# The residual of a convolution-attention layer: from TensorE transposes to a second load that VectorE turns over, with the input normalised two strips at a time

## The chip, the cores and the metric

The kernel runs on one core of one Trainium2 chip. The metric is the device time of one execution in microseconds; the times compared are medians of several executions.

## The reference, cut to what matters

The input `x` has 256 channels on a 64 x 64 image, 4096 tokens, in float32. Three stages follow one another, and each adds to a residual stream.

```python
# layer 0: group normalisation, box-window linear attention, projection
x = x + _L0_conv_ref(_gn(x), Wq, Wk, Wv, Wout, bout)
#   k, q = sigmoid(W x);  v = W x, normalised per head;  windows of 64, 32 and 16
#   out  = einsum(q, box(k v)) / (einsum(q, box(k)) + 1e-6);  Wout out + bout
# layer 1: attention and a mixture of 8 experts on tokens
t = _to_tokens(x)                      # [4096 tokens, 256 channels]
t = t + _L1_attn_ref(_ln_t(t), ...)
t = t + _L1_ffn_ref(_ln_t(t), ...)
```

What concerns this change is `x + ... + bout`: the residual, in float32, is the plain input with the output bias of the first layer added, and later stages want it with tokens on the partitions, while `x` arrives with channels on the partitions.

## The kernel before, in words

One function computes all three stages in order, and tiles of SBUF and PSUM come from pools. A scheduler decides the order of the instructions on each engine from the order in which they are written and from its own estimate of when they become ready. Each engine then works through its own queue strictly in that order and waits on semaphores. When a tile reuses the buffer of an older one (the same `tag` in a pool), its first writer waits for the older tile's last reader.

**Layout.** The image is cut into 8 strips of 8 columns (`NCH`, `SW`) and 4 blocks of 16 rows (`NB`, `BH`). A strip in a block has 128 pixels, one tile of tokens; tile `4 * strip + block` of `t` (128 tokens by 256 channels and 8 more columns) holds the residual. `act` holds the normalised input, channels on partitions, strip after strip.

**The start (L232 to L294).** `x` is loaded in eight pieces of 512 KB over two DMA queues (L237). The residual is built at once (L243 to L266): GpSimd gathers a block's pixels strip by strip into `block` (L248), TensorE transposes 128 x 128 squares into PSUM against the identity (L256), and the result goes to `t` with the bias row `bout` added: for the first two blocks by VectorE (L263), for the other two by a ScalarE copy (L265) and a GpSimd addition (L266). Beside this, VectorE takes the statistics of each channel (`bn_stats`, L273; `bn_aggr`, L274), TensorE averages them over groups of 8 channels (L276, L284), and VectorE normalises `x` into `act` with one instruction for each half of the channels (L287), all strips in one.

**prepare(g)**, called for the two groups of four heads. L309 to L332: for four tiles at a time, which is one strip, eight products of `act` with the weights of k and v (L314) fill a pair of PSUM banks; ScalarE's sigmoid takes k (L322), VectorE copies v (L323), GpSimd squares it (L324), VectorE sums the squares (L325). Every 16 tiles a square root (L328), a reciprocal (L330) and a multiplication (L332) normalise v. Three such pairs of banks (`two_banks`, L300) are used in turn, here and in all that follows in `prepare`.

Then, strip by strip (L418 to L442), products with constant matrices give running sums of k over an area of the image (L422, L426), which VectorE adds to what came before (L430, L433, L435). After the first strip TensorE also sums k times v over each cell of 64 pixels, in 512 small products (`sum_cells`, L360); ScalarE copies these to `st` (L369), and VectorE works on them between the area blocks (L378 to L398, the generator `near`). L341 then projects q and k by channel, with ScalarE's sigmoid behind (L348), into `qk`. That tile has the tag of `x`, so it takes the buffer that `x` had. ScalarE and VectorE form differences of the areas (`tall`, L464 to L469), VectorE multiplies them by q (L488), and L491 sums these products into the denominators.

**After that**, `attend` computes the window attention and adds each result to `t` (L714); attention on tokens follows, and then the experts and the output.

Of the kernel before, what the change touches and what calls it, by code (L numbers as in the profile page):

```python
# [10 lines left out]

# [1 line left out]

# [1 line left out]

# [5 lines left out]
F32 = mybir.dt.float32  # L23
BF16 = mybir.dt.bfloat16
I32 = mybir.dt.int32
AF = mybir.ActivationFunctionType
ALU = mybir.AluOpType
# [3 lines left out]
P = 128  # L31
C = 256
KC = C // P
N = 4096
NT = N // P
CH = 512
NCH = N // CH
IMG = 64
SW = 8
BH = 16  # L40
NB = IMG // BH
CELL = SW * SW
D = 32
# [68 lines left out]
def tile_conv_attn_hybrid(ctx: ExitStack, tc: tile.TileContext, a: dict, out: bass.AP):  # L112
    nc = tc.nc
# [32 lines left out]
    def row_on_all(name, n, pool):  # L146
        got = pool.tile([P, n], F32, name=f"{name}_all")
        nc.scalar.dma_start(got, a[name].partition_broadcast(P))
        return got
# [36 lines left out]
    with ExitStack() as phase:  # L186
# [23 lines left out]
        with (  # L210
            tc.tile_pool(name="c_x", bufs=1) as small,
            psum("c_ps0", 2) as ps,
        ):
            bank, _ = banks(ps)
            cst.update(constants_of("c", small))
            group = cst["group"]

            def masks(to, ys, n, kind):
                xm = cst["xmask"][:, SW * kind : SW * (kind + 1)]
                nc.gpsimd.tensor_mul(  # L220
                    to.rearrange("p n (y c) -> p (n y) c", c=SW),
                    ys.unsqueeze(2).to_broadcast([P, SW * n, SW]),
                    xm.unsqueeze(1).to_broadcast([P, SW * n, SW]),
                )

            for kind in range(2):
                masks(mask[:, kind], cst["ymask"], ncell, kind + 1)
            masks(mask0, cst["ymask"][:, SW * _MCELL0[-1] :], _MCELLS[-1], 0)
            masks(ycut, cst["ycut"], 2, 0)


            x = big.tile([P, KC, N], F32, tag="qk", name="x")  # L232
            xr = a["x"].rearrange("(k p) n -> p k n", p=P)
            for i in range(4):
                for k in range(KC):
                    at = slice(i * N // 4, (i + 1) * N // 4)
                    (nc.sync if k else nc.scalar).dma_start(x[:, k, at], xr[:, k, at])  # L237
            bout = row_on_all("L0_conv_bout", C, wts)
            first = weights(0)
            ck = constants_of("k", wts)  # L240


            ximg = x.rearrange("p k (y x) -> p k y x", x=IMG)  # L243
            tb = t.rearrange("p (i b) c -> p b i c", b=NB)
            for b in range(NB):
                block = small.tile([P, KC, NCH, P], F32, name="block", bufs=2)
                for k in range(KC):
                    nc.gpsimd.tensor_copy(  # L248
                        block[:, k].rearrange("p i (y c) -> p y i c", c=SW),
                        ximg[:, k, BH * b : BH * (b + 1), :].rearrange("p y (i c) -> p y i c", c=SW),  # L250
                    )
                for ix in range(0, NCH, 2):
                    tp = bank("tp")
                    for i in range(2):
                        for k in range(KC):
                            nc.tensor.transpose(  # L256
                                tp[:, C * i + P * k : C * i + P * (k + 1)], block[:, k, ix + i, :], ident
                            )

                    to, tp = tb[:, b, ix : ix + 2, :C], tp.rearrange("p (i c) -> p i c", c=C)  # L260
                    by = bout.unsqueeze(1).to_broadcast([P, 2, C])
                    if b < NB // 2:
                        nc.vector.tensor_add(to, tp, by)  # L263
                    else:
                        nc.scalar.copy(to, tp)  # L265
                        nc.gpsimd.tensor_add(to, to, by)  # L266


            stats = small.tile([P, KC, NCH, 6], F32, name="stats")
            mv = small.tile([P, KC, 2], F32, name="mv")  # L270
            for k in range(KC):
                for i in range(NCH):
                    nc.vector.bn_stats(stats[:, k, i, :], x[:, k, chunk(i)])  # L273
                nc.vector.bn_aggr(mv[:, k, :], stats[:, k].rearrange("p i s -> p (i s)"))  # L274
            mean_ps = bank()
            nc.tensor.matmul(mean_ps[:, :KC], group, mv[:, :, 0], start=True, stop=True)  # L276
            mean = small.tile([P, KC], F32, name="mean")
            nc.vector.tensor_copy(mean, mean_ps[:, :KC])
            off = small.tile([P, KC], F32, name="off")
            nc.vector.tensor_sub(off, mv[:, :, 0], mean)  # L280
            nc.vector.tensor_mul(off, off, off)
            nc.vector.tensor_add(off, off, mv[:, :, 1])
            var_ps = bank()
            nc.tensor.matmul(var_ps[:, :KC], group, off, start=True, stop=True)  # L284
            rstd = rstd_of(small, var_ps[:, :KC], KC, 1e-5)
            for k in range(KC):
                nc.vector.tensor_scalar(  # L287
                    act[:, k].rearrange("p (i y c) -> p y i c", y=IMG, c=SW),
                    x[:, k].rearrange("p (y i c) -> p y i c", y=IMG, c=SW),
                    mean[:, k : k + 1],  # L290
                    rstd[:, k : k + 1],
                    op0=ALU.subtract,
                    op1=ALU.mult,
                )  # L294

        def prepare(g, prep, ps):

# [11 lines left out]
            for i4 in range(0, NT, 4):  # L309
                pr = two_banks()  # L310
                kv = pr.rearrange("p j (i n o) -> p (j i) n o", i=2, n=2)
                for i in range(4):
                    for k in range(KC):
                        nc.tensor.matmul(  # L314
                            kv[:, i],
                            act[:, k, tok(i4 + i)],
                            w3[:, k, 1:3, :],
                            start=k == 0,
                            stop=k == KC - 1,
                        )  # L320
                at = slice(i4, i4 + 4)
                nc.scalar.activation(kt[:, at, :], kv[:, :, 0, :], AF.Sigmoid)  # L322
                nc.vector.tensor_copy(v[:, at, :], kv[:, :, 1, :])  # L323
                nc.gpsimd.tensor_mul(sq[:, at, :], v[:, at, :], v[:, at, :])  # L324
                nc.vector.tensor_reduce(ss[:, 4 * i4 : 4 * (i4 + 4)], heads(sq[:, at, :]), AX.X, ALU.add)  # L325
                if i4 % 16 == 12:
                    half = slice(4 * (i4 - 12), 4 * (i4 + 4))
                    nc.scalar.sqrt(ss[:, half], ss[:, half])  # L328
                    nc.vector.tensor_scalar_max(ss[:, half], ss[:, half], 1e-12)
                    nc.vector.reciprocal(ss[:, half], ss[:, half])  # L330
                    to = heads(v[:, i4 - 12 : i4 + 4, :])
                    nc.vector.tensor_mul(to, to, ss[:, half].unsqueeze(2).to_broadcast([P, 2 * NT, D]))  # L332

            qk = big.tile([P, 2, N], F32, tag="qk", name="qk")

            def by_channel(n, i):

# [80 lines left out]
            for ix in range(NCH):  # L418
                pr = two_banks()
                for m in range(NB):  # L420
                    lhsT = kt[:, NB * ix + m, :]
                    nc.tensor.matmul(  # L422
                        pr[:, 0, P * m :], lhsT, ck["before8"][:, : CH - P * m], start=m == 0, stop=m == NB - 1
                    )
                    n = SW + IMG + 1
                    nc.tensor.matmul(  # L426
                        pr[:, 1, :n], lhsT, ck["sides"][:, n * m : n * (m + 1)], start=m == 0, stop=m == NB - 1
                    )
                left = side.unsqueeze(2).to_broadcast([P, IMG + 1, SW])
                nc.vector.tensor_add(  # L430
                    area[:, ix, :IMG, :], pr[:, 0, :].rearrange("p (y c) -> p y c", c=SW), left[:, :IMG]
                )
                nc.vector.tensor_add(area[:, ix, IMG, :], pr[:, 1, :SW], left[:, IMG])  # L433
                upto = new_side()
                nc.vector.tensor_add(upto, pr[:, 1, SW:n], side)  # L435
                side = upto
                if ix == 0:

                    sum_cells()
                for _ in range(3 if ix else 0):  # L440
                    next(steps, None)
            for _ in steps:  # L442
                pass
            for i in range(0, NCH, 2):
                by_channel(0, i)
            later = [lambda i=i: by_channel(1, i) for i in range(0, NCH, 2)]
# [672 lines left out]
    with ExitStack() as phase:  # L1119
# [49 lines left out]
        with ExitStack() as routing:  # L1169
# [7 lines left out]
            at = 0  # L1177
# [303 lines left out]
```

## Time and profile before

The median of three runs is 2946.89 us (2946.64 to 2948.19). The profiled execution spans 2947.3 us.

| Engine | busy, us | share of the span |
|---|---|---|
| TensorE | 2807.9 | 95% |
| VectorE | 2079.4 | 71% |
| ScalarE | 1526.5 | 52% |
| GpSimd | 740.8 | 25% |

A share is an average over stages, so the first 140 us, to which the change belongs, are also read as stretches. Here are the busy microseconds of each engine and the clock granted to TensorE, as a part of full speed.

| stretch, us | TensorE | VectorE | ScalarE | GpSimd | clock |
|---|---|---|---|---|---|
| 20 to 34 | 11.05 | 12.22 | 6.12 | 11.17 | 0.76 |
| 34 to 62 | 28.00 | 12.55 | 8.56 | 13.33 | 1.00 |
| 62 to 78 | 12.80 | 5.65 | 3.79 | 1.04 | 0.79 |
| 78 to 97 | 19.00 | 16.52 | 3.33 | 0.00 | 1.00 |
| 97 to 140 | 37.26 | 29.41 | 13.45 | 0.00 | 0.95 |

The first stretch has the transposes and the normalisation, the second the products for k and v, the third the cell sums, the fourth the areas, and the last the projections and denominators. A row of the timeline shown further on gives the start, the time from the first start to the last end of a merged group, the engine, the line, the operation, the result and its sources with their shapes, and the number of instructions; in brackets stands the idle time before it and what ended it. PEld is TensorE's weight load. A row of the windows gives the stretch and its length, then each engine's busy time with its number of instructions (PE, PEld, VectorE, ScalarE, GpSimd), then the clock, the DMA share and GB/s.

### The profile page before, as it was taken

How to read it: one execution, taken by the hardware profiler on the slowest of the kernel's cores; microseconds unless marked ns; L12 is line 12 of the kernel's file. 1: busy time of each engine (PE TensorE's matmuls, PEld its weight loads, DVE VectorE, ACT ScalarE, POOL GpSimd, SP SyncE). 2: the span in 40 equal slices, each digit the busy share in tenths (PEclk: the TensorE clock that was granted, in tenths of full speed). 3: DMA queues.
4: the chain of work that ended last, by engine and by line, in shares of the span. 5: the costliest groups of instructions: out<-in, count | busy, mean ns of one | idle time of the engine just before them, and what ended most of it. 6: DMA issues, size and time to landing. Idle time of an engine off the chain costs nothing.

```text
span 2947.3 us, 63169 instructions
## 1 busy us (share of the span) xinstructions
PE 2807.9 (95%) x26422; PEld 1359.9 (46%) x26422; DVE 2079.4 (71%) x2975; ACT 1526.5 (52%) x2110; POOL 740.8 (25%) x832
## 2 busy tenths in 40 slices
PE   7899999889999989999999999999999689999996
PEld 5456442645644354222222222222222268888884
DVE  5776777577676886999999999999999821111113
ACT  2242324124232312888888888888888622222222
POOL 4085758108585711000000000000000022222220
PEclk9999999999999999999999999999999879999997
DMA  2000000000000000000000000000000155665665
GB/s 86 6 2 4 3 2 2 7 1 3 3 2 3 1 18 1 1 8 6 5 5 5 5 5 5 5 5 5 5 5 5 41 190 189 197 196 188 190 202 197
DMA packets 92634, 133.29 MB, mean 45 GB/s; under 512 B 16914, under 2 KB 73976, under 8 KB 92340
## 3 DMA queue, kind: packets, MB, share of 16 engines
q1 hardware_dynamic: 78008, 101.12, 10.5%
q0 software_dynamic: 6912, 18.88, 2.3%
q10 hardware_dynamic: 7420, 9.15, 0.9%
q8 instruction: 211, 3.46, 0.5%
q14 instruction: 83, 0.68, 0.1%
HBM read 111.00 MB, written 18.12 MB: 44 GB/s over the span
## 4 chain that ended last, share of the span: by engine, by line
PE 57%; DVE 1%; DMA 1%; ACT 1%; issue 1%; POOL 0%; SPq 0%; POOLq 0%; ACTq 0%; DVEq 0%
PE ps_two L970 20%; PE ps_acc L938 17%; PE ps_hp L1395 9%; PE ps_yp L1402 8%; PE ps_den L919 1%; PE ps_den L938 1%; DMA y<-yrows 1%; PE ps_tp L1370 1%; PE ps_acc L1319 1%; ACT z L1203 1%; DVE t L1439 0%; DVE total L987 0%; DMA yrows<-y,target 0%; DVE rec L1016 0%; DMA xs<-zrows,source 0%
## 5 line engine op out<-in xcount | busy, mean ns | idle before, releaser
L980 ACT ACTIVATE pe<-ps_two 128x1024 f32<-128x1024 f32 x1024 | 993.2, 1022 | 153.9 <-PE ps_two L970 148.7
L987 DVE TENSOR_TENSOR total<-total,pe 128x1024 f32<-128x1024 f32 x928 | 1058.1, 1215 | 3.3 <-ACT pe L980 3.3
L970 PE MATMUL ps_two<-qk 32*128 32x512 f32 x4096 | 631.8, 641 | 3.1 <-POOLq L925 1.9
L938 PE MATMUL ps_acc<-pe,v 128*32 128x512 f32 x4096 | 548.2, 606 | 0.1
L533 ACT COPY sm<-ps_sc 128x384 f32<-128x384 f32 (+4 forms) x486 | 232.5, 512 | 464.7 <-PE ps_sc L657 270.1
L537 POOL TENSOR_TENSOR sm<-sm,mask 128x192 f32<-128x192 f32 (+3 forms) x460 | 379.5, 860 | 231.3 <-ACT sm L533 230.8
L970 PEld LDWEIGHTS ps_two<-qk 32*128 32x128 f32 x4096 | 205.4, 183 | 420.4 <-PE ps_two L970 225.5
L537 DVE TENSOR_TENSOR sm<-ps_sc,mask 128x384 f32<-128x384 f32 (+3 forms) x708 | 323.9, 517 | 93.3 <-PE ps_sc L657 91.8
L1396 ACT ACTIVATE hid<-ps_hp,cols 128x256 f32<-128x256 f32 x288 | 136.3, 473 | 382.6 <-PE ps_hp L1395 369.9
L1245 POOL MEMSET on<- 128x256 f32 x1 | 0.3, 311 | 1179.0 <-PE ps_den L938 1179.0
L938 PEld LDWEIGHTS ps_acc<-pe,v 128*32 128x32 f32 x4096 | 80.8, 108 | 390.9 <-issue 377.7
L1395 PE MATMUL ps_hp<-xe,w 128*128 128x256 f32 x1152 | 257.0, 381 | 0.0
L1402 PE MATMUL ps_yp<-w,hid 128*128 128x256 f32 x1152 | 254.6, 379 | 0.0
L657 PE MATMUL ps_sc<-qk 32*128 32x192 f32 (+3 forms) x2688 | 245.1, 446 | 4.7 <-DVE sm L537 2.9
L1402 PEld LDWEIGHTS ps_yp<-w,hid 128*128 128x128 f32 x1152 | 216.4, 190 | 28.1
L1395 PEld LDWEIGHTS ps_hp<-xe,w 128*128 128x128 f32 x1152 | 208.4, 190 | 42.1 <-ACT hid L1396 5.2
L673 PE MATMUL ps_acc<-sm,v 128*32 128x192 f32 (+3 forms) x2688 | 217.4, 424 | 0.8 <-POOL sm L537 0.8
L1374 DVE TENSOR_SCALAR xe<-ps_tp,cols 128x256 f32<-128x256 f32 x72 | 35.8, 540 | 248.7 <-PE ps_tp L1370 228.6
L537 POOL TENSOR_TENSOR sm<-sm,ycut 128x384 f32<-128x384 f32 (+4 forms) x150 | 150.8, 1026 | 145.1 <-ACT sm L533 144.9
L657 PEld LDWEIGHTS ps_sc<-qk 32*128 32x128 f32 x2688 | 126.5, 187 | 123.6 <-DVE sm L537 69.8
L537 DVE TENSOR_TENSOR sm<-ps_sc,ycut 128x512 f32<-128x512 f32 (+4 forms) x250 | 127.4, 561 | 70.7 <-PE ps_sc L588 68.9
L1404 DVE TENSOR_TENSOR y<-ps_yp,b 128x256 f32<-128x256 f32 x72 | 30.6, 425 | 208.0 <-PE ps_yp L1402 207.9
(235 smaller groups left out, 2279.3 us busy)
## 6 DMA issues: line engine op xcount, KB each, us to landing
w<-in_L_ffn_W SPq DMA_DIRECT2D x72, 1024.0 KB
b<-in_L_ffn_b SPq DMA_DIRECT2D x36, 128.0 KB
zrows<-z SPq DMA_DIRECT2D x4, 1024.0 KB
y<-yrows SPq DMA_DIRECT2D x8, 512.0 KB
y<-yrows ACTq DMA_DIRECT2D x8, 512.0 KB
rec<-recs SPq DMA_DIRECT2D x60, 64.0 KB
x<-in_x ACTq DMA_DIRECT2D x4, 512.0 KB
x<-in_x SPq DMA_DIRECT2D x4, 512.0 KB
```

What stands on the lines that cost most here:

```text
L533: nc.scalar.copy(sm[:, :used], sc[:, :used])
L537: engine.tensor_mul(to, of, mk.unsqueeze(1).to_broadcast(list(to.shape)))
L657: nc.tensor.matmul(scs[h][:, at : at + n], kT[hs[h], tok(i)], qT[hs[h], CH * ix + CELL * c0 : CH * ix + CELL * c1], start=True, stop=True, ...
L673: nc.tensor.matmul(acc[hs[h], CELL * c0 : CELL * c1], v[:, i, hs[h]], sms[h][:, at : at + n], start=not begun[0], stop=last and at == plac ...
L938: nc.tensor.matmul(to[D * hd : D * (hd + 1), :], lhsT(hd), rhs[:, hd, :], start=start, stop=stop, skip_group_check=True,)
L970: nc.tensor.matmul(sc[hd // 2][:, hd % 2, :], qk[hs, 1, g, tok(i)], qk[hs, 0, g, chunk(qc)], start=True, stop=True,)
L980: nc.scalar.activation(pe[:, pair, :], s, AF.Exp, scale=C**-0.5)
L987: add = nc.vector.tensor_add(to, first[:, pair, :] if i == 1 else to, pe[:, pair, :])
L1374: nc.vector.tensor_scalar(xe[:, k, :], tp[:, k, :], cols[:, gain], cols[:, shift], op0=ALU.mult, op1=ALU.add,)
L1395: nc.tensor.matmul(hp, w1[:, k, tok(n)], x_now[:, k, :], start=k == 0, stop=k == KC - 1)
L1396: nc.scalar.activation(hid[:, n, :], hp, AF.Gelu, bias=cols[:, n : n + 1])
L1402: nc.tensor.matmul(yp, hid[:, n, tok(j)], w2[:, n, :], start=n == 0, stop=n == NH - 1)
```

## The change

The residual no longer passes through TensorE. It is built from a second load of `x` into `rows`, whose layout lets 32 x 32 blocks be turned over in place of whole 128 x 128 squares: partition `32 q + c` holds, for each row block `b` and each `j`, four image rows of channel `32 j + c`. VectorE's transpose then swaps 32 channels with 32 pixels in each block and yields a tile of `t` per instruction. The bias is wanted per partition in this layout, so it is loaded as a column for each `j`, and ScalarE adds it in place. `rows` takes the buffer of `x` once the normalisation has read it, and `qk`, whose allocation moves down, takes it after that. The aim is to take the transposes, the gathering and the bias additions out of the start, so that nothing but statistics and normalisation stands before the products for k and v, and to put the residual where VectorE waits for the cell sums. To that end `issue_after` fixes the order on an engine: ScalarE's bias blocks 0 and 1 stand before the last two sigmoids, VectorE's blocks 0 to 2 follow the last normalisation of v and precede the second area block, and block 3 stands between the fifth and the sixth.

Two smaller parts: the normalisation is written as eight instructions, two strips and one half of the channels each, so that the first products can begin after two of them; and a square root of a constant early on loads ScalarE's table for it before `rstd` needs it.

```diff
-            bout = row_on_all("L0_conv_bout", C, wts)
...
-            for b in range(NB):
-                block = small.tile([P, KC, NCH, P], F32, name="block", bufs=2)
...
+            bout = wts.tile([P, C // D], F32, name="bout")
+            for q in range(4):
+                nc.scalar.dma_start(
+                    bout[D * q : D * (q + 1), :], a["L0_conv_bout"].rearrange("(j c) -> c j", c=D)
+                )
+            root = small.tile([P, 1], F32, name="root")
+            nc.scalar.sqrt(root, ident[:, :1])
...
-            for k in range(KC):
-                nc.vector.tensor_scalar(
-                    act[:, k].rearrange("p (i y c) -> p y i c", y=IMG, c=SW),
...
+            for i in range(0, NCH, 2):
+                for k in range(KC):
+                    nc.vector.tensor_scalar(
+                        act[:, k].rearrange("p (i y c) -> p y i c", y=IMG, c=SW)[:, :, i : i + 2, :],
...
+        rows = big.tile([P, NB, C // D, 4 * IMG], F32, tag="qk", name="rows")
+        for b in range(NB):
+            for q in range(4):
+                nc.sync.dma_start(
+                    rows[D * q : D * (q + 1), b],
+                    a["x"].rearrange("(j c) (b q f) -> b q c j f", c=D, b=NB, q=4)[b, q],
                 )
+        def biased(b):
+            for j in range(C // D):
+                last = nc.scalar.activation(rows[:, b, j], rows[:, b, j], AF.Identity, bias=bout[:, j : j + 1])
+            return last.ins
+        def residual(b):
+            for i in range(NCH):
+                last = nc.vector.transpose(
+                    t[:, NB * i + b, :C].rearrange("p (j c) -> p j c", c=D),
+                    rows[:, b].rearrange("p j (y i c) -> p j y i c", y=4, c=SW)[:, :, :, i, :],
+                )
+            return last.ins
...
+                with ExitStack() as order:
+                    if not g and i4 >= NT - 8:
+                        order.enter_context(tc.issue_after(biased((i4 - NT + 8) // 4)))
+                    nc.scalar.activation(kt[:, at, :], kv[:, :, 0, :], AF.Sigmoid)
...
+            if not g:
+                biased(2)
+                biased(3)
...
-            qk = big.tile([P, 2, N], F32, tag="qk", name="qk")
...
+                with tc.issue_after(turned) if ix in (1, 5) and not g else nullcontext():
+                    nc.vector.tensor_add(
+                        area[:, ix, :IMG, :], pr[:, 0, :].rearrange("p (y c) -> p y c", c=SW), left[:, :IMG]
+                    )
...
+                if not g and ix in (0, 4):
+                    for b in range(NB - 1) if ix == 0 else (NB - 1,):
+                        with tc.issue_after(latest.ins):
+                            turned = residual(b)
```

## The prediction

> **What bounds the kernel now.** I read the page first: shares by engine, then the chain that ended last.
>
> ```profile
> PE 57%; DVE 1%; DMA 1%; ACT 1%; issue 1%; POOL 0%; SPq 0%; POOLq 0%; ACTq 0%; DVEq 0%
> ```
>
> TensorE carries the chain, so the change can only gain where TensorE starts late or waits. All edits lie in the first 110 us, so I read the timeline there.
>
> ```profile
> 17.25 1.27 DVE L263 TENSOR_TENSOR t<-ps_tp,L_conv_bout_all 128x512 f32<-128x512 f32 x2
> 18.44 0.68 DVE L273 BATCH_NORM_STATS2 stats<-x 128x6 f32<-128x512 f32 x1
> ...
> 24.85 0.95 DVE L281 TENSOR_TENSOR off<-off 128x2 f32<-128x2 f32 x1
> ...
> 25.83 1.19 DVE L282 TENSOR_TENSOR off<-off,mv 128x2 f32<-128x2 f32 x1
> ...
> 28.34 5.70 DVE L287 TENSOR_SCALAR act<-x,mean,rstd 128x4096 f32<-128x4096 f32 x2
> ...
> 33.80 27.89 PE L314 MATMUL ps_two<-w,act 128*128 128x256 f32 x128 [0.68 <-ACT t L265]
> ```
>
> The residual's adds sit between the statistics (L263 before the last L273); two-column operations take 0.95 and 1.19 us while GpSimd adds to `t`; and the k/v products (L314) wait for the whole normalisation and the last transposes. They then run without a gap to 61.7. The next loss is at the cell sums:
>
> ```profile
> 66.61 2.29 DVE L332 TENSOR_TENSOR v<-v,ss 128x2048 f32<-128x2048 f32 x1
> ...
> 68.96 1.45 PE L360 MATMUL ps_two<-v,kt 64*32 64x32 f32 x133 [0.92 <-DVE v L332]
> ...
> 72.59 1.50 PE L360 MATMUL ps_two<-v,kt 64*32 64x32 f32 x123 [2.18 <-issue]
> ...
> 74.06 1.93 ACT L369 COPY st<-ps_two 128x1024 f32<-128x1024 f32 x2 [8.88 <-PE ps_two L360]
> ...
> 76.02 0.43 DVE L378 TENSOR_TENSOR st<-st 128x256 f32<-128x256 f32 x1 [7.12 <-ACT st L369]
> ```
>
> TensorE waits 0.92 us there for `v`, then 2.18 us for nothing but issue, and VectorE idles 7.12 us until ScalarE has copied the sums. The view by windows gives the clock after such pauses:
>
> ```profile
> 28.00:30.00 2.00, 2.00 (x10) 1.71 (x10) 1.83 (x2) 1.17 (x3) 0.91 (x2) 0.50 0.00 0
> 74.00:76.00 2.00, 2.00 (x13) 1.26 (x5) 0.00 (x0) 1.93 (x2) 0.00 (x0) 0.50 0.00 0
> ```
>
> It is 0.50 in both (the third figure from the end), and back at 1.00 some 4.6 us after work resumed at 72.59.
>
> [...]
>
> **The change, part by part.** *Removed before the k/v products:* 64 transposes, 8 GpSimd copies (8.0 us), 16 evacuations or adds on VectorE and ScalarE, 8 GpSimd adds (13.2 us). *Statistics:* the last bn_stats starts at 17.25 and ends its share at 17.85 (pitch 0.60: nine took 5.45); aggregate 0.36: 18.2. Two small products at 0.6 each (27.08 to 27.70 in the trace), one copy 0.2, three two-column operations at 0.16 (the eight-column L433 takes 0.155), and add, square root, reciprocal 0.64 (27.70 to 28.34; the root's table is now loaded earlier, in idle ScalarE time): rstd at about 20.9. *Normalisation by two strips:* 4096 elements took 2.41 us undisturbed, so 1024 take about 0.16 + (2.41 - 0.16)/4 = 0.7. TensorE needs two of the eight: it starts at about 22.3 instead of 33.8, **11.5 us earlier**. The other six (about 4 us) run ahead of it, since one strip's eight products take 3.5 us. The build's order of DMA issues lets the k and v weights start about 15 instead of 12 us, still before 22.3. The new bias loads are tiny, ahead of idle ScalarE time: nothing.
>
> *Clock:* TensorE was warm at 33.8 from the transposes; now it comes out of near idleness. About 5 us at half clock lose **2.5 us**. The k/v products end at about 52.7, 9.0 earlier.
>
> *Second load:* 4 MB in 1 KB pieces, queued behind the normalisation's last read (about 26), each issue also behind one eight loads earlier. The last stage reads 1 KB rows at about 350 GB/s[...]. That is 12 to 19 us plus about 2: all there at 40 to 48. ScalarE wants the first quarter at about 42 and the second at 50. Hidden.
>
> *Bias on ScalarE:* 32 activations of 256 elements with one bias pointer. [...]the nearest row, with two pointers, has 0.588. I take 0.40 each, 3.2 us a block. Sigmoids come every 3.5 us and take 0.6, so the 13 us fit, except the block ahead of the last sigmoid (about 0.3 us late). Behind that sigmoid wait VectorE's `v`, GpSimd's square and the norm. The third block ends at about 60, before the copies of the cell sums are wanted; the fourth comes after them. `v` is normalised at about 60.2 instead of 68.9.
>
> *Turning on VectorE:* 24 transposes of 256 elements between the norm and the first area evacuation, 8 more before the sixth. [...] I take 0.34 to 0.36: 8.4 us, so VectorE is free at 68.6, where it used to begin its sums at 76.0. Behind them wait the area evacuations, and for those TensorE's third PSUM buffer: with three buffers in rotation TensorE can run to the fourth strip first. From here VectorE has about 18.8 us of its old work (16.5 of 19 us in the 78 to 97 window were busy) and 2.8 us of transposes: the last area evacuation ends at about 90.5, 7.4 earlier than 97.9.
>
> *TensorE in this stretch:* the new order puts all of the second area block between the halves of the cell sums, which fills the 0.92 us wait. If instruction supply kept up, six area blocks (3.05 each) from 64.7 would end at 83.0; the q products (13.9) then wait a little for ScalarE's `tall` copy, table load and first sigmoid (4.2 us after the last evacuation, as at 97.8 to 102.0), ending at 98.5 against 110.49: 12 us. But the 2.18 us issue gap has its likeliest cause in 512 tiny matmuls back to back, and those remain (the second head group shows 5.9 us of such gaps at 573 to 581). I keep it, with half of the slow clock after it, 1.2 us, less what the `tall` wait covers: q products end at about 100.5.
>
> **Sum.** 11.5 - 2.5 - 0.3 + about 1.3 for the better-filled cell sums = **10.0 us**. From 110 us on both builds have the same order on every engine, and TensorE leads, so all of it reaches the end: 2946.9 - 10.0 = **2936.9**.
>
> **Rivals.** (1) *VectorE becomes the bound.* At 0.61 us a transpose the 32 cost 8.3 us more; the `tall` copy and the q products follow almost one for one, since VectorE's slack is about 1 to 2 us. Gain 10.0 - 6.5 = 3.5: **2943.4**. For it: strided eight-element runs at the source, never seen in this trace; and VectorE is already 87% busy in the 78 to 97 window.[...] (2) *A DMA wait on ScalarE takes the transposes' place.* The biased rows stand in ScalarE's queue ahead of the sigmoids that empty PSUM. If the second quarter came at 66 instead of 50, TensorE would stop with all buffers full: 16 us lost against 10 gained, **2953**, slower. That needs 2.1 MB at about 55 GB/s from 26 on; the trace's 350 GB/s for 1 KB rows speaks against it[...]. Transposes of 0.95 us would end there too (32 x 0.6 = 19 us more, less 2 to 3 of slack). (3) *Only noise is left:* a longer slow clock, new issue gaps and slower eight-element normalisation runs take 5 to 8 us: about **2945**.
>
> **Numbers.** Forecast 0.66, rival 1 0.16, rival 2 0.07, rival 3 0.11. 0.2% is 5.9 us, so faster means under 2941.0: the forecast, and a little of rival 1, 0.77; same 0.16; slower 0.07. Range: below, 2933, where neither the issue gap nor the slow clock costs anything in the cell sums; above, 2944, which takes in rival 1.
>
> **What would show it.** In the profile of the changed kernel: the first k/v product at 21.5 to 23.5 and its clock at 0.5 for about 5 us; act's eight instructions at about 0.7; no sigmoid waiting for a load; transposes at about 0.42 with a pitch of 0.35; no wait of the area products longer than 1 us on VectorE; the first product into the denominator at 98 to 101. Wrong if the transposes last over 0.5 us, if `rows` lands after 50, or if TensorE waits for area evacuations.

## The result, and the profile after

The changed kernel takes 2936.6 us (median of 6 runs, 2933.1 to 2939.1), the kernel before 2946.8 us (6 runs, 2942.7 to 2948.2). The ratio is 0.9968, with a 95% interval of 0.9955 to 0.9981: 5.6 to 13.3 us faster. The forecast of 2936.9 us is met to 0.3 us. The profile shows that this is partly luck: two steps of the sum were wrong by about 5 us each, with opposite signs.

The page of the changed kernel: busy time by engine, and the chain that ended last.

```profile
PE 2794.7 (95%) x26358; PEld 1352.3 (46%) x26358; DVE 2083.2 (71%) x3005; ACT 1533.0 (52%) x2134; POOL 720.3 (25%) x816
...
DMA 1%; DVE 0%; issue 0%; PE 0%; ACT 0%; ACTq 0%; POOLq 0%; DVEq 0%
```

This time the chain breaks off within the last per cent, so it says nothing about the start; TensorE is 95% busy, as before. The timeline of its start answers the lines of the prediction (start, duration, engine, line, output and inputs, count, and in brackets the wait with what ended it). VectorE first:

```profile
21.96 5.87 DVE L271 TENSOR_SCALAR act<-x,mean,rstd 128x1024 f32<-128x1024 f32 x8
...
57.94 2.29 DVE L344 TENSOR_TENSOR v<-v,ss 128x2048 f32<-128x2048 f32 x1
60.15 7.95 DVE L298 STREAM_TRANSPOSE t<-rows 128x256 f32<-128x256 f32 x24
...
72.42 0.43 DVE L392 TENSOR_TENSOR st<-st 128x256 f32<-128x256 f32 x1 [3.54 <-ACT st L383]
```

And TensorE in the same stretch:

```profile
22.87 29.94 PE L322 MATMUL ps_two<-w,act 128*128 128x256 f32 x128 [1.58 <-issue]
...
60.01 0.68 PE L374 MATMUL ps_two<-v,kt 64*32 64x32 f32 x55 [2.37 <-issue]
...
69.67 0.81 PE L374 MATMUL ps_two<-v,kt 64*32 64x32 f32 x71 [2.42 <-issue]
71.52 2.08 PE L436 MATMUL ps_two<-cstk,kt 128*128 128x512 f32 x2 [1.04 <-ACT st L383]
```

The k/v products start at 22.87 in place of 33.80, and the area products behind them (L436) at 52.65 in place of 61.53. The second half of `v` is normalised at 60.2, and 24 transposes take 7.95 us, 0.33 us each. But the cell sums now show two issue gaps (idle time for which the profile shows nothing that ended it), 2.37 and 2.42 us, where there was one of 2.18. The windows (length, busy time of PE, PEld, DVE, ACT and POOL, then the clock, DMA share and GB/s) show what follows:

```profile
24.00:26.00 2.00, 2.00 (x7) 1.55 (x6) 2.00 (x4) 0.00 (x0) 0.00 (x0) 1.00 0.00 0
...
28.00:30.00 2.00, 2.00 (x11) 1.74 (x11) 0.78 (x2) 0.60 (x1) 0.00 (x0) 1.00 0.49 144
...
62.00:64.00 2.00, 2.00 (x8) 1.39 (x6) 2.00 (x7) 0.00 (x0) 0.00 (x0) 0.50 0.00 0
...
72.00:74.00 2.00, 2.00 (x5) 0.97 (x5) 0.43 (x1) 2.00 (x6) 0.00 (x0) 0.50 0.00 0
```

The clock falls to 0.50 after each gap, at 62 us and again at 72. At 24 us the products come at half pace, 0.43 us apart, 7 in two microseconds in place of 11. The view prints a clock of 1.00 there because TensorE's clock record has no entry yet: its first one, to full clock, stands at 27.1 us, and from then on the products come 0.22 us apart.

Four points of the run, in two traces of each kernel (the second ones are e1 and e2 below), give the time at which each begins:

| | before | after | gain of the means |
|---|---|---|---|
| first product into the denominator | 110.5, 108.8 | 105.4, 104.1 | 4.9 us |
| output projection of the first head group (L710, now L731) | 520.9, 519.2 | 510.0, 507.2 | 11.5 us |
| score products of 128 columns, second head group (L588, now L609) | 746.2, 743.5 | 733.2, 731.7 | 12.4 us |
| first score products of the token attention (L970, now L991) | 1158.5, 1155.5 | 1147.4, 1147.2 | 9.7 us |

So half of the 10 us is gained where the code changed. The other half appears between 110 and 510 us, where TensorE's queue is unchanged, and some 3 us of it go back after 740 us, which no experiment here followed up. The experiments ask what the first part was worth, and where the second comes from. From here on "the stretch" is the time from the first product into the denominator to that output projection.

### The profile page after: what moved, and what is told of

The parts are those of the page before. It is cut to its first block, busy times and chain, and to the rows that moved or that the text cites. A ratio compares the mean times of both kernels' runs of the same rounds, so it can differ in the third digit from the quotient of the medians.

```text
span 2935.2 us, 63107 instructions
## 1 busy us (share of the span) xinstructions
PE 2794.7 (95%) x26358; PEld 1352.3 (46%) x26358; DVE 2083.2 (71%) x3005; ACT 1533.0 (52%) x2134; POOL 720.3 (25%) x816
## 3 DMA queue, kind: packets, MB, share of 16 engines
q1 hardware_dynamic: 82360, 105.31, 10.9%
q8 instruction: 210, 3.44, 0.5%
## 5 line engine op out<-in xcount | busy, mean ns | idle before, releaser
L991 PE MATMUL ps_two<-qk 32*128 32x512 f32 x4096 | 629.1, 639 | 3.6 <-POOLq L946 1.9
L991 PEld LDWEIGHTS ps_two<-qk 32*128 32x128 f32 x4096 | 204.8, 183 | 418.7 <-PE ps_two L991 222.2
L1425 DVE TENSOR_TENSOR y<-ps_yp,b 128x256 f32<-128x256 f32 x72 | 30.6, 425 | 208.1 <-PE ps_yp L1423 208.1
```

The lines of the kernel that those rows point to most:

```text
L991: nc.tensor.matmul(sc[hd // 2][:, hd % 2, :], qk[hs, 1, g, tok(i)], qk[hs, 0, g, chunk(qc)], start=True, stop=True,)
```

## The experiments

### The same kernels again, and the normalisation alone

*e1 and e2: no edit.*

> The changed kernel once more, unedited, for a second trace. Theory A (the later gain is chance): the front stretch up to the first product into the denominator again gains about 5 us (105.4 in the first trace), but the further 7 us that the first pair of traces shows between 110 us and the end change size or place by several us from one trace to the other, since nothing that code after 110 us does was changed; the ratio stays near 0.9968. Theory B (the later gain is systematic[...]): the second trace shows the same gains in the same places (about 1.5 us in the attention of 248 to 312 us, 3.5 us at 410 to 460 us, 1 to 2 us in the second head group's preparation) to within 1 us.

> The kernel before once more, unedited, for a second trace. Theory A (chance): its gaps of TensorE without a reason but issue differ from those of its first trace by several us in all, at other places. Theory B (systematic): the same gaps in the same places; the product into the denominator starts at 110.5, the second head group's k/v products end at 565.8 and attention ends at 2321, each within 1 us. Time 2946.8, ratio 1.000 with an interval under 0.15% in both.

Measured: e1 2938.7 us, 0.9962 (0.9949 to 0.9976); e2 0.9996 (0.9988 to 1.0004). The stretch lasts 410.4 us in both traces of the kernel before, 404.6 and 403.0 us in those of the changed one. The gaps stand at the same products in both traces of a kernel. The start varies: the first product into the denominator came 1.7 us earlier in e2 than in the first trace, where theory B allowed 1 us. But the 6 us behind it are systematic; chance (theory A) is out.

*e3: the changed kernel with the old normalisation.*

```diff
-for i in range(0, NCH, 2):
-    for k in range(KC):
-        nc.vector.tensor_scalar(act[... i : i + 2 ...], ...)
+for k in range(KC):
+    nc.vector.tensor_scalar(act[:, k]..., ...)      # all strips
```

> The changed kernel with the normalisation of x in its old two whole instructions in place of eight. Theory A (the early start of the k/v products is what gains): they start about 4.3 us later, at 27.2, and nothing behind gives it back: 4 us slower than the changed kernel, so a ratio near 0.998. Theory B (TensorE's first products run at half clock and the cell sums' gaps swallow the lead anyway): under 1.5 us.

Measured: 2938.3 us, 0.9962 (0.9948 to 0.9975), the changed kernel's own ratio in e1. Its timeline, VectorE's normalisation and then TensorE:

```profile
21.00 4.74 DVE L270 TENSOR_SCALAR act<-x,mean,rstd 128x4096 f32<-128x4096 f32 x2
...
23.52 29.27 PE L319 MATMUL ps_two<-w,act 128*128 128x256 f32 x128 [3.18 <-issue]
52.62 1.02 PE L433 MATMUL ps_two<-cstk,kt 128*128 128x512 f32 x2
```

TensorE started at 23.52, as soon as the first half of the channels was normalised, and not at 27. In this kernel's TensorE queue six of the 128 products stand ahead of the first one that waits for the second half, and at the slow pace of the start, 0.43 us each, they fill the time until VectorE has done that half at 25.7. The area products begin at 52.6, against 51.5 in e1, which had the same statistics time: the split is worth 1.1 us there and nothing that the total time shows. That is theory B's size, with a reason that neither theory named.

*e4: the kernel before with the new normalisation alone,* the reverse of that edit.

> The kernel before with nothing changed but the normalisation, in eight instructions of two strips. Theory A (the split pays only once TensorE has no transposes of the residual ahead of the k/v products): the transposes end at about 33, so the k/v products start at 33 in place of 33.8, and the time stays within 0.8 us: ratio 0.9997 to 1.000. Theory B (the split gains by itself): 3 to 5 us faster.

Measured: 0.9999 (0.9991 to 1.0007); the k/v products start at 34.30 (33 was expected). As theory A says, the split does nothing while the residual's transposes stand ahead.

### Where do the 6 us after 110 us come from?

The gaps' places give the idea. In the second head group's cell sums, whose code is the same in both kernels, TensorE's timeline of the kernel before reads:

```profile
573.17 0.50 PE L360 MATMUL ps_two<-v,kt 64*32 64x32 f32 x36 [1.98 <-issue]
...
577.09 1.29 PE L360 MATMUL ps_two<-v,kt 64*32 64x32 f32 x128 [1.47 <-issue]
580.85 0.67 PE L360 MATMUL ps_two<-v,kt 64*32 64x32 f32 x38 [2.47 <-issue]
```

and that of the changed kernel:

```profile
561.94 1.03 PE L374 MATMUL ps_two<-v,kt 64*32 64x32 f32 x98 [2.23 <-issue]
...
565.78 1.56 PE L374 MATMUL ps_two<-v,kt 64*32 64x32 f32 x128 [0.47 <-issue]
569.25 1.26 PE L374 MATMUL ps_two<-v,kt 64*32 64x32 f32 x100 [1.90 <-issue]
```

Gaps come 128 products apart, and their places have moved by 62 products. The change removed 64 products, the transposes, ahead of them. The list of DMA queues on the page of after has one of instructions, with 210 packets and 3.44 MB, 16.4 KB a packet. If a packet held 128 products with their 128 weight loads, the distance of the gaps, TensorE's 26358 products and as many weight loads would fill 206 of them, an estimate from that distance and the page's count of products:

```profile
q8 instruction: 210, 3.44, 0.5%
```

That makes a new theory, P: TensorE's instructions come in such packets, and a gap stands where one of them ends and its products were done before the next had come; the change moved TensorE's packet borders by half a packet. The next three kernels move the borders; the products that they add lie in idle time of TensorE at the start.

*e5: the kernel before with 32 small products at the head of TensorE's queue;* in the profile they are 64 products with 64 weight loads. *e6: the changed kernel with the same 32. e7: with 64.*

```diff
 mean_ps = bank()
+for _ in range(32):                                  # e7: 64
+    nc.tensor.matmul(mean_ps[:32, 64:96], ident[:64, :32], ident[:64, :32], start=True, stop=True)
```

> The kernel before with 32 tiny products (32x32, none is read) at the head of TensorE's queue, where it waits for the first block anyway until 13.2 us. They are 64 product records with 64 weight loads, half of the 128 that lie between two issue gaps of the cell sums (gaps after the last 166, 38 of the second head group's sums are 128 apart), and half of a 16 KB packet of the instruction queue. Theory P (the gain after 110 us comes from where the borders of the instruction packets fall in TensorE's program, which the removed 64 transposes moved by half a packet): the gaps move to the places they have in the changed kernel (98 of the second head group's sums left after one, not 36 or 38) and the stretch from the first product into the denominator to the end of the first head group's attention falls from 410.3 us to about 404.3: 6 us faster than before, ratio 0.998, with no other change at all. Theory Q (it comes from another engine's work, GpSimd's or ScalarE's, that the change took away): no gain, ratio 1.000.

> The changed kernel with 32 such tiny products ahead of its statistic products, where TensorE is idle until 18.4 us. Theory P: the borders come back to where the kernel before has them, the stretch from the first product into the denominator to the end of the first head group's attention rises from 404.3 to about 410.3 us, and the time with it: 6 us slower than the changed kernel, ratio near 0.9985. Theory Q: no change, ratio 0.9962.

> The control to it: 64 tiny products, so 128 records with their weight loads, a whole packet. Theory P: the borders fall where they fall in the changed kernel, the same time as it, ratio 0.996 to 0.997. If added products cost by themselves, or if any shift does harm, it is as slow as the one with 32, or slower.

| | first product into the denominator | the stretch | ratio to before |
|---|---|---|---|
| before (two traces) | 110.5, 108.8 | 410.4, 410.4 | |
| e5, before and half a packet | 112.2 | 406.0 | 0.9990 (0.9982 to 0.9999) |
| after (two traces) | 105.4, 104.1 | 404.6, 403.0 | 0.9968, 0.9962 |
| e6, after and half a packet | 101.1 | 409.9 | 0.9955 (0.9942 to 0.9969) |
| e7, after and a whole packet | 104.2 | 405.8 | 0.9958 (0.9944 to 0.9971) |

Half a packet, 64 products, moves the gaps to the other kernel's places and a whole one, 128 products, leaves them. In the second head group e6 has 34 and 36 products after its gaps, as the kernel before has 36 and 38; e7 has 98 and 100, as the changed kernel has. The timeline of e6:

```profile
563.49 0.43 PE L376 MATMUL ps_two<-v,kt 64*32 64x32 f32 x34 [2.25 <-issue]
...
571.63 0.66 PE L376 MATMUL ps_two<-v,kt 64*32 64x32 f32 x36 [2.74 <-issue]
```

and of e7:

```profile
561.92 1.03 PE L376 MATMUL ps_two<-v,kt 64*32 64x32 f32 x98 [2.14 <-issue]
...
569.25 1.19 PE L376 MATMUL ps_two<-v,kt 64*32 64x32 f32 x100 [2.33 <-issue]
```

The trace also times the packets of that queue. In the changed kernel one of them runs from 57.42 to 58.56 us, and TensorE goes on at 60.01; another runs from 66.97 to 68.24, and TensorE goes on at 69.67. It is so at all 55 issue gaps in the cell sums of both head groups, over the fourteen traces of this study: one packet of this queue ends 1.2 to 1.6 us before TensorE goes on, whether the gap lasts 0.16 or 2.74 us. I read that as TensorE waiting there for the arrival of instructions. Which instructions a packet holds, the trace doesn't say.

The stretch follows: 409.9 to 410.4 us with one placing of the borders, 403.0 to 406.0 with the other, whatever the kernel. In the groups of instructions from 237 to 525 us (busy time and mean ns, then the idle time before them) one line shows the largest change. In the kernel before:

```profile
L619 PE MATMUL ps_acc<-sm,v 64*32 64x192 f32 (+5 forms) x1280 | 48.6, 376 | 5.8 <-issue 5.5
```

and in the changed one:

```profile
L640 PE MATMUL ps_acc<-sm,v 64*32 64x192 f32 (+5 forms) x1280 | 45.6, 375 | 0.6 <-issue 0.6
```

With its neighbours in the loop (L588 and L607, now L609 and L628) the idle time before these three groups is 8.0 us before and 4.8 us after. Over the whole stretch TensorE is idle for 18.5 us before and 14.5 after (18.0 and 13.3 in the second traces). The rest, 1.9 and 2.6 us, is busy time of the same number of products; what shortens it isn't settled.

The total times, however, fell otherwise than theory P's expectation had them. e6 is not 6 us slower, because its start is 3.7 us faster than the changed kernel's: it loses less to gaps in its first cell sums. Its timeline there:

```profile
63.35 1.45 PE L376 MATMUL ps_two<-v,kt 64*32 64x32 f32 x128 [1.74 <-issue]
66.80 0.33 PE L376 MATMUL ps_two<-v,kt 64*32 64x32 f32 x7 [2.00 <-issue]
67.06 2.07 PE L438 MATMUL ps_two<-cstk,kt 128*128 128x512 f32 x2
```

Both gaps fall in the second half of the sums, so the slow products of the half clock come once, behind 67.06. In the changed kernel they come twice, as shown. e5 is the mirror: its stretch gains 4.5 us, its start loses 2.6, although its k/v products begin at 31.43, earlier than in the kernel before. The borders were traded between two places. I had expected the places to move and forgot that the first cell sums have borders too.

### What do the residual and VectorE cost now?

*e8: the changed kernel without the second load, the bias and the transposes;* the residual and its bias are left out, and zeros stand in `t`.

```diff
+nc.gpsimd.memset(t[:, :, :C], 0.0)
-        nc.sync.dma_start(rows[...], ...)
-    nc.scalar.activation(rows[:, b, j], ..., AF.Identity, bias=...)
-    nc.vector.transpose(t[...], rows[...])
```

> The changed kernel without the second load, the bias and the 32 transposes: the residual's half of t is set to 0 by GpSimd at the start, so the residual and its bias are left out. Theory A (as predicted: load, bias and transposes lie beside other work, VectorE then still waits for ScalarE's copy of the cell sums): within 1 us of the changed kernel, ratio 0.996. Theory B (the residual still costs, by VectorE or by the order of ScalarE's queue): 2 us faster or more, ratio under 0.9955.

Measured: 2935.8 us, 0.9958 (0.9944 to 0.9971); first product into the denominator at 104.2. Theory A: where they lie now, these parts cost nothing that can be measured. TensorE's order in the cell sums is not quite the same in this kernel, and it loses 5.6 us to gaps there in place of 4.8, so a cost of about 1 us could be hidden.

*e9: each transpose done twice.*

```diff
 for i in range(NCH):
-    last = nc.vector.transpose(...)
+    for _ in range(2):
+        last = nc.vector.transpose(...)
```

> The changed kernel with each of its 32 transposes done twice, as if one took 0.67 us in place of 0.33: 10.6 us more for VectorE. Theory A (VectorE has slack there: it waits 3.5 us for ScalarE's copy of the sums and 3.6 us for TensorE, which itself loses time to issue gaps): the slack of about 7 us takes most of it, 1 to 4 us slower than the changed kernel, ratio 0.9970 to 0.9975. Theory B (rival 1 of the prediction, VectorE as the bound: each added us on VectorE comes through): 8 to 10 us slower, ratio near 0.999.

Measured: 2936.6 us, 0.9962 (0.9948 to 0.9977), no slower at all. Of its timeline, a line of VectorE and two of TensorE:

```profile
59.56 15.76 DVE L298 STREAM_TRANSPOSE t<-rows 128x256 f32<-128x256 f32 x48
...
90.70 13.95 PE L355 MATMUL ps_two<-act,w 128*128 128x512 f32 x32
104.58 1.06 PE L512 MATMUL ps_mm<-prod,cstk 128*32 128x512 f32 x8
```

VectorE is busy 7.8 us longer at 59 to 75 and 2.6 us longer later, and the first product into the denominator comes at 104.58 as ever. The slack is at least the 10.4 us added, more than either theory said. VectorE as the bound, rival 1 of the prediction, is out. But the slack is then nearly used up: from 59 to 102 us VectorE waits only 0.4 us.

### Without the gaps

*e10: the cell sums in four parts, one behind each of the first four area blocks, in both head groups.* The four blocks share one PSUM tile while the sums hold the other two, and the transposes go a block at a time behind the evacuations.

```diff
-                pr = two_banks()
+                if ix not in (1, 2, 3):
+                    pr = two_banks()
...
-                if ix == 0:
-                    sum_cells()
+                if ix < 4:
+                    with tc.issue_after(covered.ins):      # this block's last product
+                        summed = sum_cells(sp, ix)         # 8 of the 32 tiles; block ix + 1 is queued behind
-                if not g and ix in (0, 4):
-                    for b in range(NB - 1) if ix == 0 else (NB - 1,):
-                        ... turned = residual(b)
+                if not g and 0 < ix < 5:
+                    ... turned = residual(ix - 1)
```

> The changed kernel with the cell sums of both head groups in four parts of 128 product records, each put behind one of the first four area blocks, which share one PSUM tile, and the transposes a block at a time behind the second to fifth evacuation. Theory P ([...]sums back to back wait, and with an area block of 3.05 us between them they don't): no issue gap over 0.7 us and no slow clock in either head group's sums; the first product into the denominator at 96 to 98 in place of 104.8, 3 to 5 us more in the second head group, 9 to 13 us in all: ratio near 0.9925. Theory V (VectorE is the bound there as soon as TensorE has no gaps): the area products wait for evacuations, the first product into the denominator at 101 or later, under 5 us gained, ratio 0.9945 or more.

Measured: 2923.0 us, 0.9917 (0.9901 to 0.9932), the fastest kernel of the study: about 13 us less than the changed kernel (0.9968 - 0.9917, or 0.9962 - 0.9917 against e9, on the same chip). TensorE's timeline:

```profile
54.26 1.29 PE L374 MATMUL ps_two<-v,kt 64*32 64x32 f32 x128
55.79 1.13 PE L443 MATMUL ps_two<-cstk,kt 128*128 128x512 f32 x2 [0.24 <-DVE side L458]
...
81.31 15.66 PE L355 MATMUL ps_two<-act,w 128*128 128x512 f32 x36
96.90 1.07 PE L520 MATMUL ps_mm<-prod,cstk 128*32 128x512 f32 x8
```

and its group of cell sums from 50 to 110 us:

```profile
L374 PE MATMUL ps_two<-v,kt 64*32 64x32 f32 x512 | 5.2, 200 | 0.0
```

The same 512 products, with no idle time before them (4.8 us in the changed kernel), and the clock stays at 1.00 from 51 to 81 us. The first product into the denominator comes at 96.9; the second head group gains too, 0.7 us of gaps in place of 4.6. Theory P holds. VectorE keeps up: TensorE's one wait for it is the 0.24 us shown. It is busy for 8.76 of the 9 us from 72 to 81, though, so e9's slack is not shown for this kernel.

*e11: the same four parts in the kernel before,* with e5's 32 small products so that the borders fall as in e10.

> The kernel before with the same four parts of the cell sums, and with 32 tiny products at its start so that its packet borders fall as in the changed kernel. What the change itself is worth once neither kernel loses time to instruction supply is the difference between this and the changed kernel with four parts. Theory A (the prediction's terms for the start, 11.5 - 2.5 - 0.3 us, hold and the issue gaps alone hid them): no issue gap in the sums, the first product into the denominator at 105 to 107, against 96.9 there, so 8 to 10 us slower than the changed kernel with four parts: ratio near 0.9947. Theory B (the change is worth only the 5 us seen at that point): 101 to 103, 4 to 6 us slower: ratio near 0.9935.

Measured: 0.9945 (0.9931 to 0.9958), k/v products from 33.98 to 61.9, and no gap in its first cell sums. The first product into the denominator comes at 105.5, against 96.9 in e10: 8.6 us, theory A. But e10's queue has 36 q products ahead of it, as shown above, and this kernel's has 32, as all others but e12's:

```profile
91.65 13.95 PE L344 MATMUL ps_two<-act,w 128*128 128x512 f32 x32
```

The q products begin at 91.65 and at 81.31, 10.3 us apart. This is what the change is worth at that point when the borders are taken out of the comparison. At the output projection it is 10.6 us (510.1 against 499.5), and in the total times about 8 (0.9945 against 0.9917).

*e12: e10 with 64 products of 96 columns ahead of the statistics, to keep TensorE at work.*

```diff
 mean_ps = bank()
+for _ in range(64):
+    nc.tensor.matmul(mean_ps[:, 64:160], ident, ident[:, :96], start=True, stop=True)
```

> The changed kernel with four parts and 64 products of 96 columns (none is read) at the head of TensorE's queue, a whole packet, from 4.4 us to about 17.5, so that TensorE comes to the k/v products from work. Theory A (their slow start, 29.7 us for products that take 27.9 in the kernel before, is the half clock after idleness): the k/v products take 27.9 again and end 1.8 us earlier, 1.5 to 2 us faster than without: ratio near 0.991. Theory B (the pauses around the two statistic products alone bring the half clock back, or the loads of the first weights slow them): 29.7 as before, no gain, ratio 0.9917.

Measured: 2925.2 us, 0.9915 (0.9901 to 0.9928), no gain. TensorE's timeline:

```profile
4.59 16.81 PE L260 MATMUL ps_mm<-cst 128*128 128x96 f32 x128 [4.59 <-DMA cst<-in_constants]
...
24.35 30.60 PE L324 MATMUL ps_two<-w,act 128*128 128x256 f32 x128 [1.58 <-issue]
```

and the window of TensorE at 24 us (length, busy time, clock, DMA share, GB/s):

```profile
24.00:26.00 2.00, 1.65 (x4) 0.50 0.00 0
```

The added products ran until 21.4 and not 17.5, so the k/v products start 2.4 us later than in e10. They are slow all the same, 30.6 us: from 23.1 to 29.9 us the clock was at 0.50 again, from within the second of two pauses, 0.84 and 1.58 us, around the second statistic product. Whether work up to the first k/v product would help stays open.

## Why the prediction was right, and where it was not

**Statistics and start.** Forecast: k/v products from 22.3. They began at 22.87 and 21.98 in the two traces. The eight instructions of the normalisation come 0.73 us apart (5.87 for the eight, one of them 0.81). ScalarE's table load ahead of the root, 1.28 us at 25.76 in the kernel before, stands at 10.85, and the root runs at 21.52 without one. Right; but the credit for the split was not earned: e3 starts only 1.5 us later than e1 without it, and is as fast.

**Slow pace of the start.** 2.5 us allowed; 29.94 us in place of 27.89 is 2.05, and from 22.87 to the clock's return at 27.1 are 4.2 us at half pace, forecast 5. The end of the k/v products, forecast at 52.7, is at 52.8. The prediction read the recovery after the gap in the kernel before as 4.6 us; the clock was back at 77.8, 5.2 us after 72.59.

**Second load, bias, transposes.** The load ran at 208 GB/s between 30 and 45 us. The 12 us of the forecast are 4.2 MB at the 350 GB/s that 1 KB rows reached in the last stage (347 to 364 from 2910 to 2925 us of the trace of before); its 19 us, and with them the 48, rest on no row of that trace. The load ended at 49 to 50 us, forecast 40 to 48, and no activation waited for it. Eight bias activations take 3.29 us, 0.41 us apart and 0.50 for one alone; forecast 0.40, which no row gave. The transposes come 0.33 apart and one lasts 0.40. The forecast of 0.34 can be had from the trace of before: 0.42 for a row of 256 elements (L381) less the 0.08 by which neighbours overlap at `bn_stats`. Rival 1's 0.61 is an estimate as well: it adds to the 0.34 once more what those 256 elements take beyond the 0.155 of L433's eight. That they cost nothing measurable is shown by e8. The slack of VectorE, "1 to 2 us" in rival 1, was far too small (e9).

**The cell sums: the term that failed.** The sum kept the one gap of 2.18 us and half of a slow clock, 1.2 us: 3.4. The changed kernel loses 9.2 us there: 4.8 of gaps, 1.0 waiting for ScalarE's copy of the sums that end so late, and 3.4 of slow area products (27.0 and 11.5 us for its two groups of area products, against 24.2 and 10.9 in e10). From the first area product to the first product into the denominator it takes 52.75 us, against 48.96 in the kernel before; the sum had this part 1.3 shorter, not 3.8 longer. So the first product into the denominator came at 105.4 and not at 100.5, a gain of 4.9 in place of 10.0. I had named the cause, 512 tiny products back to back, but took the gap as a fixed price of one. It has a place: in these traces the gaps stand 128 products apart, and removing 64 transposes moved those of both head groups' sums.

**"From 110 us on ... all of it reaches the end": failed too, the other way.** The same shift took 6 us out of the first head group's attention.

**Hence the time.** The two misses cancel. With the borders where the kernel before has them (e6), the gain is 8.6 us at the first product into the denominator, 9.1 at the output projection and 10.1 at the token attention: the forecast's course, nearly. So the mechanism of the forecast is what the change does, at 8.6 of its 10.0 us by e6 and at 10.3 by e11 and e10, and the border terms happened to balance. Of the rivals, 1 and 2 fell. Rival 3 was in part what happened at the start, 5 us left there, though not by noise.

## What to carry to other kernels

Before a forecast that removes or adds instructions ahead of a tiny-product stretch, count where the issue gaps stand in the trace: if they come at a constant number of instructions, expect the edit to move them, as 64 products moved them here (e5, e6), in both head groups' sums. To compare two versions fairly, pad the shorter queue by the difference, or cure the gaps: with the short products mixed with long ones, gaps of 0.7 us were left of 9.4 in the two head groups (e10), and this was worth more than the change studied. And when a term lets work start earlier by cutting an instruction up, look in the build's queue for what the consumer can do in the meantime (e3).

## What the runs showed of the hardware that I had not expected

- **Tiny products back to back had an issue gap every 128 products.** In the cell sums of e5 and e6 and the kernel before, stretches of 128 products that take 1.3 to 1.5 us come every 3.4 to 4.1 us (573.17 to 577.09 to 580.85 in the kernel before, for one), with 1.5 to 2.7 us of it idle. TensorE goes on 1.2 to 1.6 us after the end of a packet of the instruction queue. The same 512 products between longer ones have no gap in the first head group (e10).
- **The half clock came with pauses of 0.84 to 2.37 us:** a gap of 2.37 us amid tiny products in the changed kernel (0.50 from 61.2 us), and in e12 pauses of 0.84 and 1.58 us around one short product (0.50 from 23.1, within the second). What share the short products themselves have in it was not separated.
- **The entries of the clock record lie multiples of 3.41 us apart.** In each of the fourteen traces all entries of TensorE's clock record are whole multiples of 3.41 us apart: 27.08, 61.22, 64.63, 71.46 and 74.87 in the changed kernel. The slow start of the k/v products ends at such an entry, after 4.2 us in this trace, 3.7 in e1, 3.0 in e10 and 5.5 in e12, and they take 29.94, 29.69, 29.33 and 30.60 us, against 27.89 in the kernel before.
